# Six groups of TensorE sums in six PSUM banks instead of three groups in each of two

## The chip, the cores and the metric

The kernel runs on one core of a Trainium2 chip. The metric is the device time of one execution in microseconds (us); lower is better. Engines are called as in the profile: PE is TensorE's matmul, PEld its weight load, DVE is VectorE, ACT is ScalarE, POOL is GpSimd, SP is SyncE, which issues the stores. PSUM is the memory that matmuls write to. It has eight banks here, each with room for 512 fp32 numbers on each of 128 partitions.

## The reference, cut to what matters

Inputs are `xi` and `xj`, each 1024 x 39 x 16 (batch, field, element). For each of the 741 pairs of fields (row, column with column < row), each batch entry gets the 16 x 16 outer product of two vectors. It is normalised with a mean and a variance per pair, over the batch and both elements, and multiplied by a 16 x 16 weight:

```
cross = xj[:, rows, :, None] * xi[:, cols, None, :]
mean = jnp.mean(cross, axis=(0, 2, 3), keepdims=True)
var = jnp.mean(jnp.square(cross - mean), axis=(0, 2, 3), keepdims=True)
normed = (cross - mean) * jax.lax.rsqrt(var + BN_EPS)
normed = normed * gamma[None, :, None, None] + beta[None, :, None, None]
out = normed[:, :, None, :, :] * W[None, None, :, :, :]
```

The output is 1024 x 1 x 741 x 16 x 16 in fp32, 777 MB, so the bulk of the run is the writing of it. But nothing of the output can be finished before the mean and variance are known, and these need the whole batch.

## The kernel before, in words

The batch is laid out as 128 partitions x 8 entries; the index of the entry is called t (0 to 7). The kernel has two phases.

**Statistics.** The mean of an outer product is a product of sums: for each batch entry and field, the kernel needs only the sum over the 16 elements of `xi` and of `xj` (k = 0), and the same sum of their squares (k = 1). These sums are called moments. ACT makes the squares (`square`, L361), one field tensor and one t at a time. Then the 16 elements have to be summed, in four ways:

- `reduce` (L364): DVE sums 608 numbers per partition to 38.
- `fold` (L368) and `folded` (L371): POOL adds the upper eight elements to the lower eight, and DVE sums what is left, 304 numbers to 38.
- `matrix_sums` (L380) and `take` (L386): PE multiplies by a unit matrix and accumulates in PSUM, four of the 16 elements at a time for one t, or two at a time for two t's, so that 152 numbers per partition are left; DVE sums these to the moments. This serves k = 0 for t = 1 to 5. The groups are called `i_1`, `j_1` (t = 1), `i_23`, `j_23` (t = 2 and 3) and `i_45`, `j_45` (t = 4 and 5); `i` stands for `xi`, `j` for `xj`. For k = 0, t = 0 and 7 go by `reduce`, t = 6 by `fold` and `folded`; for k = 1 nearly all goes by `reduce`.
- `gram` (L390): PE multiplies the moments of `xj` with those of `xi` over the batch and so gets a 38 x 38 table of sums for k = 0 and one for k = 1.

All this is in a hand-written order (`tc.manual_schedule()`): each engine executes its instructions in the order in which the program lists them, and the waits between engines follow from the tiles and banks that they share. On PE the order is `i_1`, `j_1`, `i_23`, `j_23`, `i_45`, `j_45`, then the `gram` matmuls. On DVE, 28 summing instructions come one after the other: 22 reductions from SBUF with the six `take`s between them. The lines that place the groups and the first `take`s are

```
at = 2 * T * G * (n // 2)
ps = banks[5 + x][:, at : at + 2 * T * G]
...
i_1 = matrix_sums(1, 1, 2)
j_1 = matrix_sums(0, 1, 2)
i_23 = matrix_sums(3, 2, 4)
j_23 = matrix_sums(2, 2, 4)
reduce(1, 1, 1)
take(*i_1)
```

so the three `i` groups lie side by side in bank 6, the three `j` groups in bank 5, and the matmuls of `i_23` and `j_23` stand in the program ahead of `take(*i_1)`.

After the two tables, a short chain on 38 x 38 numbers gives scale and offset of each pair: ACT L461 and L462, DVE L463 to L466, ACT L468, DVE L471 to L474. `spread` (L488) copies a table row to all 128 partitions with a matmul, and `apply` (L499 to L506) multiplies with gamma and adds beta. While the statistics run, POOL and ACT also make the raw outer products of the first output tile (L150 and L148).

**Output.** The output is made in tiles: one row of the pair table and two t's each. POOL scales `xi` (L170), ACT and POOL make outer products (L148, L150), DVE adds the offset and multiplies by the weight (`finish`, L308) with a share of POOL and ACT, and SP issues the store (L231). The first tile is different: it has raw products, which get scale and offset in `affine` (ACT L245, POOL and DVE L247) and the weight in `weigh` (L254), whose first store is the kernel's first. The output lies in one large SBUF buffer (`y_sb`) used as a ring: a later tile can be written only when an earlier one's store is done.

PSUM holds the banks `ps_s` (bank 0, written by twelve warm-up matmuls at the start, L402), `ps_c` (bank 1, small tables of the chain), `ps_g` (banks 2 to 4; the first two take the tables of `gram`), banks 5 and 6, and one more bank for `w_dve`, a copy of the weight that ACT makes at L469. `spread` uses banks 5, 6 and 2 to 4 later on.

Of the kernel before, what the change touches and what calls it, by code (L numbers as in the profile page):

```python
# [14 lines left out]
T = 2  # L15
# [26 lines left out]
def tile_pair_outer_batchnorm(  # L42
# [49 lines left out]
    w_dve = psp.tile([P, 1, EE], F32, name="w_dve")  # L92
# [27 lines left out]
    G = F - 1  # L120
# [9 lines left out]
    banks = [psp.tile([P, 512], F32, name=f"ps{n}") for n in range(7)]  # L130
    ps_s, ps_c, ps_g = banks[0], banks[1], banks[2:5]
# [186 lines left out]
    with tc.manual_schedule():  # L318
# [44 lines left out]
        def reduce(x, k, t):  # L363
            nc.vector.tensor_reduce(moment(x, k, t, t + 1), field(x, k)[:, t : t + 1], AX.X, ALU.add)  # L364
# [7 lines left out]
                moment(x, k, t, t + 1), halves[k][x][:, t : t + 1], AX.X, ALU.add  # L372
            )

        def matrix_sums(n, t0, t1):
            x, q = n % 2, 2 * T // (t1 - t0)
            at = 2 * T * G * (n // 2)
            ps = banks[5 + x][:, at : at + 2 * T * G]
            for e in range(0, E, q):
                nc.tensor.matmul(  # L380
                    ps, unit, sources[x][:, t0:t1, :, e : e + q], start=e == 0, stop=e + q == E
                )
            return x, t0, t1, ps.rearrange("p (t f q) -> p t f q", t=t1 - t0, q=q)

        def take(x, t0, t1, ps):
            nc.vector.tensor_reduce(moment(x, 0, t0, t1), ps, AX.X, ALU.add)  # L386
# [23 lines left out]
        reduce(1, 1, 0)  # L410
        reduce(0, 0, 0)
        reduce(0, 1, 0)
        i_1 = matrix_sums(1, 1, 2)
        j_1 = matrix_sums(0, 1, 2)
        i_23 = matrix_sums(3, 2, 4)
        j_23 = matrix_sums(2, 2, 4)
        reduce(1, 1, 1)
        take(*i_1)
        reduce(0, 1, 1)
# [3 lines left out]
        reduce(1, 1, 3)  # L423
        reduce(0, 1, 3)
        take(*i_23)
        i_45 = matrix_sums(5, 4, 6)
        j_45 = matrix_sums(4, 4, 6)
        reduce(1, 1, 4)
        reduce(0, 1, 4)
        fold(1, 0, 6)  # L430
# [130 lines left out]
```

## Time and profile before

| | |
|---|---|
| time, median of 3 runs | 1872.28 us (1871.1 to 1872.44) |
| span of the profiled execution | 1869.4 us |
| busy: DVE, ACT, POOL | 92%, 84%, 83% of the span |
| busy: PE | 34.5 us, 2% |
| written to memory | 776.99 MB |
| moved, mean over the span | 419 GB/s |
| first store issued | 31.73 us after the start of the span |

A row of a profile's timeline gives the start in us, the duration of the row (first start to last end), engine, line, operation, output <- input with their shapes, the count, and in brackets how long the engine had been idle before it and what ended the wait. The letter q after an engine is its instruction queue. The names `ps` and `y_sb` stand for all banks, and for the ring buffer together with the small work areas laid into it.

### The profile page before, as it was taken

To read this page: it belongs to the slowest core of one execution; us is meant where nothing else is said; L and a number is where in the kernel's file an instruction comes from. 1 tells how busy PE (TensorE), PEld (TensorE's weight loads), DVE (VectorE), ACT (ScalarE), POOL (GpSimd) and SP (SyncE) were. 2 spreads that over 40 slices of the span, in tenths; PEclk is the share of its full clock that TensorE was granted. 3 is DMA by queue.
4 is the path that set the end of the run, shared out by engine and by line. 5 is a ranking of instruction groups with operands and counts; after the bars stand their busy time and mean duration, and the time that the engine had idled before them with its cause. 6 is when DMAs were issued, how large, how long until landed. Compare 5 with 4: busy or idle time off the path is not lost.

```text
span 1869.4 us, 9385 instructions
## 1 busy us (share of the span) xinstructions
PE 34.5 (2%) x212; PEld 32.9 (2%) x212; DVE 1714.5 (92%) x2638; ACT 1578.7 (84%) x3130; POOL 1546.0 (83%) x1655
## 2 busy tenths in 40 slices
PE   7000000000000000000000000000000000000000
PEld 7000000000000000000000000000000000000000
DVE  7999889899999999999999999999999999999994
ACT  7999888888888877666798989999999998989892
POOL 7999878777777788999988888888888888888882
PEclk7555555555555555555555555555555555555555
DMA  6999999999999999999999999999999999999998
GB/s 239 389 419 422 429 427 427 422 426 424 427 428 426 426 427 425 426 428 426 421 428 426 425 425 432 427 427 429 429 425 426 430 427 429 429 424 431 426 429 359
DMA packets 55286, 783.60 MB, mean 419 GB/s; under 512 B 4784, under 2 KB 6448, under 8 KB 18096
## 3 DMA queue, kind: packets, MB, share of 16 engines
q1 hardware_dynamic: 54928, 782.53, 98.8%
q14 instruction: 69, 0.57, 0.1%
q10 hardware_dynamic: 288, 0.48, 0.1%
q8 instruction: 1, 0.02, 0.0%
HBM read 6.00 MB, written 776.99 MB: 419 GB/s over the span
## 4 chain that ended last, share of the span: by engine, by line
DMA 53%; ACT 20%; DVE 16%; issue 2%; POOL 1%; SPq 0%; ACTq 0%; DVEq 0%; POOLq 0%
DMA out_dram<-y_sb 53%; ACT y_sb L148 20%; DVE y_sb L308 16%; POOL y_sb L150 0%; POOL xs L170 0%; SPq L231 0%; POOL y_sb L294 0%; DVE xs L183 0%; ACTq L148 0%; DVEq L556 0%; DVEq L308 0%; POOLq L294 0%; POOLq L150 0%
## 5 line engine op out<-in xcount | busy, mean ns | idle before, releaser
L308 DVE SCALAR_TENSOR_TENSOR y_sb<-y_sb,st_sb,w_dve 128x512 f32<-128x512 f32 (+1 forms) x2511 | 1653.1, 740 | 113.6 <-issue 96.0
L148 ACT ACTIVATE y_sb<-xs,xj_sb 128x144 f32<-128x144 f32 (+23 forms) x2930 | 1455.2, 600 | 236.2 <-DMA out_dram<-y_sb 181.4
L297 POOL TENSOR_TENSOR y_sb<-y_sb,w_sb 128x2048 f32<-128x2048 f32 (+3 forms) x155 | 517.6, 3346 | 89.0 <-ACT y_sb L292 79.4
L150 POOL TENSOR_SCALAR y_sb<-xs,xj_sb 128x320 f32<-128x320 f32 (+19 forms) x1006 | 559.6, 580 | 9.4 <-DMA out_dram<-y_sb 9.4
L170 POOL TENSOR_TENSOR xs<-xi_sb,st_sb 128x640 f32<-128x640 f32 (+33 forms) x135 | 184.1, 1364 | 176.4 <-ACT y_sb L148 172.2
L294 POOL TENSOR_SCALAR y_sb<-y_sb,st_sb 128x512 f32<-128x512 f32 x291 | 197.6, 694 | 5.1 <-ACT y_sb L148 5.1
L292 ACT ACTIVATE y_sb<-y_sb,st_sb 128x512 f32<-128x512 f32 x160 | 100.3, 710 | 3.8 <-POOL y_sb L150 2.1
L203 POOL TENSOR_TENSOR y_sb<-xs,xj_sb 128x1280 f32<-128x1280 f32 (+2 forms) x24 | 66.7, 2806 | 0.0
L193 DVE TENSOR_TENSOR y_sb<-xs,ps 128x256 f32<-128x256 f32 (+3 forms) x32 | 24.8, 817 | 0.6
L488 PE MATMUL ps<-y_sb 38*128 38x38 f32 (+37 forms) x76 | 16.4, 397 | 2.4 <-DVE y_sb L474 2.4
L488 PEld LDWEIGHTS ps<-y_sb 38*128 38x128 f32 x76 | 16.3, 329 | 2.5 <-issue 2.5
L247 POOL TENSOR_SCALAR y_sb<-y_sb,st_sb 128x512 f32<-128x512 f32 x9 | 7.0, 793 | 8.4 <-ACT y_sb L148 8.4
L150 POOL TENSOR_SCALAR y_sb<-xi_sb,xj_sb 128x304 f32<-128x304 f32 x24 | 12.0, 518 | 0.0
L254 DVE TENSOR_TENSOR y_sb<-y_sb,w_dve 128x2048 f32<-128x2048 f32 (+4 forms) x6 | 10.8, 1840 | 0.5 <-POOL y_sb L247 0.5
L364 DVE TENSOR_REDUCE y_sb<-y_sb 128x38 f32<-128x608 f32 x14 | 10.4, 779 | 0.0
L386 DVE TENSOR_REDUCE y_sb<-ps 128x76 f32<-128x152 f32 (+1 forms) x6 | 1.9, 313 | 6.5 <-PE ps L380 6.5
L461 ACT ACTIVATE y_sb<-ps 38x38 f32<-38x38 f32 x1 | 0.2, 198 | 8.0 <-PE ps L390 8.0
L361 ACT ACTIVATE y_sb<-xj_sb 128x608 f32<-128x608 f32 x8 | 5.7, 710 | 1.2 <-DMA xj_sb<-in_r_xj_dram 0.8
L245 ACT ACTIVATE y_sb<-y_sb,st_sb 128x512 f32<-128x512 f32 x9 | 6.5, 806 | 0.3 <-ACT y_sb L148 0.3
L361 ACT ACTIVATE y_sb<-xi_sb 128x608 f32<-128x608 f32 x8 | 5.7, 708 | 1.2 <-DMA xi_sb<-in_r_xi_dram 1.0
L380 PE MATMUL ps<-xi_sb,y_sb 128*128 128x152 f32 x40 | 5.9, 297 | 3.9 <-DVE y_sb L386 2.7
L380 PE MATMUL ps<-xj_sb,y_sb 128*128 128x152 f32 x40 | 5.7, 290 | 0.0
(40 smaller groups left out, 58.0 us busy)
## 6 DMA issues: line engine op xcount, KB each, us to landing
out_dram<-y_sb SPq DMA_DIRECT2D x16, 3072.0 KB, 21.9
out_dram<-y_sb SPq DMA_DIRECT2D x20, 2432.0 KB, 12.6
out_dram<-y_sb SPq DMA_DIRECT2D x10, 4608.0 KB, 15.2
out_dram<-y_sb SPq DMA_DIRECT2D x12, 3840.0 KB, 20.8
out_dram<-y_sb SPq DMA_DIRECT2D x16, 2816.0 KB, 22.0
out_dram<-y_sb SPq DMA_DIRECT2D x12, 3584.0 KB, 22.9
out_dram<-y_sb SPq DMA_DIRECT2D x12, 3328.0 KB, 24.3
out_dram<-y_sb SPq DMA_DIRECT2D x15, 2560.0 KB, 12.4
```

The lines of the kernel that those rows point to most:

```text
L148: nc.scalar.activation(y, src, AF.Copy, scale=scale)
L150: engine.tensor_scalar(y, src, scale, 1.0, ALU.mult, ALU.mult)
L170: nc.gpsimd.tensor_tensor(xs, xi_sb[:, t0 : t0 + T, 0:r, :], s_sb[:, :, n0 : n0 + r, :].to_broadcast([P, T, r, E]), ALU.mult,)
L193: nc.vector.tensor_tensor(view(n)[:, t].rearrange("p n (i j) -> p n i j", j=E), xs[:, t].unsqueeze(2).to_broadcast([P, r, E, E]), xj_short ...
L203: nc.gpsimd.tensor_tensor(view(n)[:, t].rearrange("p n (i j) -> p n i j", j=E), xs[:, t].unsqueeze(2).to_broadcast([P, r, E, E]), xj_sb[:, ...
L292: nc.scalar.activation(y[:, :, c, :], y[:, :, c, :], AF.Identity, bias=t_c)
L294: nc.gpsimd.tensor_scalar(y[:, :, c, :], y[:, :, c, :], t_c, 1.0, ALU.add, ALU.mult)
L297: nc.gpsimd.tensor_tensor(y[:, :, c0:c1, :], y[:, :, c0:c1, :], w_sb.unsqueeze(1).to_broadcast([P, T, c1 - c0, EE]), ALU.mult,)
L308: stt(y[:, t : t + size, c, :], y[:, t : t + size, c, :], t_sb[:, n0 + c : n0 + c + 1], w_dve.to_broadcast([P, size, EE]), ALU.add, ALU.mult,)
L361: nc.scalar.activation(squares[x][:, t], sources[x][:, t], AF.Square, scale=scales[x])
L380: nc.tensor.matmul(ps, unit, sources[x][:, t0:t1, :, e : e + q], start=e == 0, stop=e + q == E)
L488: nc.tensor.matmul(ps[:, :, first[r] - n0 : first[r] - n0 + r], pick[:, r - 1, :], stq[:, :, 0:r], start=True, stop=True,)
```

## The change

Each of the six groups gets a bank of its own. `matrix_sums` is told the bank, and the column offset goes away. The banks are ones that the program holds anyway, at a time when they are otherwise unused: `ps_c` before the chain, `ps_g[2]` before `spread`, `ps_s` after the warm-up, and the bank of `w_dve` before the weight is copied into it. The purpose is that a `take` should no longer share a bank with a group that PE writes around the same time. Number, shapes and order of the instructions on each engine stay as they are.

```diff
-        def matrix_sums(n, t0, t1):
-            x, q = n % 2, 2 * T // (t1 - t0)
-            at = 2 * T * G * (n // 2)
-            ps = banks[5 + x][:, at : at + 2 * T * G]
+        def matrix_sums(ps, x, t0, t1):
+            q = 2 * T // (t1 - t0)
+            ps = ps[:, 0 : 2 * T * G]
...
-        i_1 = matrix_sums(1, 1, 2)
-        j_1 = matrix_sums(0, 1, 2)
-        i_23 = matrix_sums(3, 2, 4)
-        j_23 = matrix_sums(2, 2, 4)
+        i_1 = matrix_sums(ps_c, 1, 1, 2)
+        j_1 = matrix_sums(ps_g[2], 0, 1, 2)
+        i_23 = matrix_sums(banks[5], 1, 2, 4)
+        j_23 = matrix_sums(banks[6], 0, 2, 4)
...
-        i_45 = matrix_sums(5, 4, 6)
-        j_45 = matrix_sums(4, 4, 6)
+        i_45 = matrix_sums(ps_s, 1, 4, 6)
+        j_45 = matrix_sums(w_dve[:, 0], 0, 4, 6)
```

The changed kernel is one line shorter, so its line numbers from `matrix_sums` on are lower by one: L379 is the matmul and L385 the `take`.

## Prediction

> **What bounds the kernel now.** I read the slices of the page first, to see whether one thing binds throughout.
>
> ```profile
> DVE  7999889899999999999999999999999999999994
> DMA  6999999999999999999999999999999999999998
> GB/s 239 389 419 422 429 427 427 422 426 424 427 428 426 426 427 425 426 428 426 421 428 426 425 425 432 427 427 429 429 425 426 430 427 429 429 424 431 426 429 359
> ```
>
> From the second slice on the DMA engines are busy throughout and move some 425 GB/s; the writing is the long bound. Only the first slice (47 us) stands out. So the second view is the busy time by stretch:
>
> ```profile
> 16.00:20.00 4.00, 3.99 (x30) 3.99 (x31) 2.03 (x3) 1.98 (x4) 3.73 (x7) 1.00 0.34 127
> 20.00:24.00 4.00, 1.93 (x26) 1.31 (x24) 3.52 (x8) 0.00 (x0) 2.03 (x5) 1.00 0.00 0
> 24.00:26.00 2.00, 0.74 (x8) 0.60 (x8) 2.00 (x5) 0.02 (x1) 0.00 (x0) 0.64 0.00 0
> 26.00:30.00 4.00, 1.32 (x7) 1.22 (x7) 2.05 (x11) 2.97 (x9) 0.00 (x0) 0.50 0.00 0
> ...
> 60.00:70.00 10.00, 0.00 (x0) 0.00 (x0) 9.97 (x18) 10.00 (x23) 9.65 (x13) 0.50 0.82 335
> ```
>
> (Columns: length, busy PE, PEld, DVE, ACT, POOL, PE clock, DMA share, GB/s.) Loads are over before 20 us; from 20 to 30 us nothing is moved. Ten us of the span are pure statistics, with no other work than some raw products beside them. Every us off this phase starts the store stream a us sooner.
>
> Third, the waits of the first 32 us, and fourth, the timelines of DVE and PE there:
>
> ```profile
> DVE y_sb L386 <- PE ps L380: 6.5, 3, 3.6
> PE ps L380 <- DVE y_sb L386: 2.7, 1, 2.7
> ```
>
> ```profile
> 6.15 1.47 DVE L364 TENSOR_REDUCE y_sb<-y_sb 128x38 f32<-128x608 f32 x2
> 11.26 0.32 DVE L386 TENSOR_REDUCE y_sb<-ps 128x38 f32<-128x152 f32 x1 [3.64 <-PE ps L380]
> 13.34 0.32 DVE L386 TENSOR_REDUCE y_sb<-ps 128x38 f32<-128x152 f32 x1 [0.38 <-PE ps L380]
> 15.65 0.31 DVE L386 TENSOR_REDUCE y_sb<-ps 128x76 f32<-128x152 f32 x1
> 20.48 0.32 DVE L386 TENSOR_REDUCE y_sb<-ps 128x76 f32<-128x152 f32 x1 [2.45 <-PE ps L380]
> 25.75 0.47 DVE L371 TENSOR_REDUCE y_sb<-y_sb 128x38 f32<-128x304 f32 x1
> ```
>
> ```profile
> 5.63 1.27 PE L380 MATMUL ps<-xi_sb,y_sb 128*128 128x152 f32 x8 [0.22 <-DMA xi_sb<-in_r_xi_dram]
> 6.74 1.20 PE L380 MATMUL ps<-xj_sb,y_sb 128*128 128x152 f32 x8
> 8.90 2.32 PE L380 MATMUL ps<-xi_sb,y_sb 128*128 128x152 f32 x16 [0.96 <-DMA xi_sb<-in_r_xi_dram]
> 11.06 2.24 PE L380 MATMUL ps<-xj_sb,y_sb 128*128 128x152 f32 x16
> 16.01 2.35 PE L380 MATMUL ps<-xi_sb,y_sb 128*128 128x152 f32 x16 [2.71 <-DVE y_sb L386]
> 18.20 2.24 PE L380 MATMUL ps<-xj_sb,y_sb 128*128 128x152 f32 x16
> ```
>
> The reader is to compare ends with starts. `i_1` is done at 5.63 + 1.27 = 6.90, yet its `take` starts at 11.26, just after the end of `i_23` (8.90 + 2.32 = 11.22). The `take` of `j_1` (13.34) follows the end of `j_23` (13.30), and that of `j_23` (20.48) the end of `j_45` (20.44). The other way round, `i_45` starts at 16.01, after the `take` of `i_23` ends at 15.96. So the waits are by bank, not by column: a `take` waits for the last group that stands ahead of it in the program in the same bank, though that is not its data.
>
> **What the Trainium skill says.** "PSUM — Partial Sum Buffer", section "PSUM bank collisions raise a hardware error", says that a matmul's write and another engine's access to one bank must be kept apart even at different columns, and that different banks are free. The four coincidences above agree. "Perfetto Trace Analysis", "Optimization Strategy", says to look at regimes apart and find gaps on the engine that limits a regime; here that is DVE before 26 us, not the DMA of the average. "DMA: Bandwidth & Descriptors", "Where 436 GB/s comes from", gives 435 GB/s as the ports' ceiling; the 425 to 429 here are near it, so the store stage can hardly catch up or go faster by itself. "TensorE: Matmul & The Clock Gate", "What's actually happening", says that the clock halves after an idle window of about 3.4 us; the trace has it falling between 24 and 26 us.
>
> **The change part by part.**
>
> 1. *Waits removed on DVE.* The three waits are 3.64 + 0.38 + 2.45 = 6.47 us. A wait also breaks overlap: reductions back to back start 0.70 us apart though one lasts 0.78 (two in 1.47), so each wait hides 0.08; three make 0.24. Bound: 6.7 us.
>
> 2. *Do the true inputs come in time?* I lay DVE's instructions out back to back from 6.15, where nothing changes yet, with the steps of the trace: 0.70 for a `reduce`, 0.23 for a `take`, 0.38 for a `folded`. After three reductions, the `take` of `i_1` starts at 7.54 (data 6.90); two reductions on, that of `j_1` at 9.16 (data 6.74 + 1.20 = 7.94); three on, that of `i_23` at 11.47 (data 11.22); three on, that of `j_23` at 13.77 (data 13.30). ACT's squares are single rows 0.7 to 0.8 apart, the one of `xi` for t = 6 starting at 13.51, for t = 7 at 15.13 and of `xj` at 15.94, each 0.71 long. Counting back, squares lead the DVE by 0.4 to 0.6 us at t = 3 to 5. POOL's folds for t = 6 end at 14.38, 15.18 and 15.96; DVE wants them at 14.7, 16.0 and 16.4. The fold for t = 7 ends at 17.56. All in time, the tightest by 0.2 to 0.5 us. The last reduction then starts at 19.05 in place of 25.75, and ends at 19.5: 6.7 us sooner.
>
> 3. *Wait removed on PE.* `i_45` no longer waits for a `take`. Its loads have landed: ACT squares t = 5 of `xi` at 11.99 and of `xj` at 12.74 without a DMA wait. So it follows `j_23`: groups of 16 rows start 2.16 to 2.19 apart (8.90, 11.06; 16.01, 18.20), which gives 13.22 for `i_45`, 15.4 for `j_45`, and an end at about 17.65 in place of 20.44. The `take`s of both come at 15.76 and 18.12, after these ends (15.57 and 17.65); 0.2 us is the margin for `i_45`.
>
> 4. *What stands behind the groups on PE.* The `gram` matmuls start at about 17.6. Before, 16 of their rows took 0.84 us from 20.85 on and the last eight, from the `take` of `j_45` on, 0.74 (25.20 to 25.94). Sixteen, six and eight rows, some 0.9, 0.3 and 0.74 us, end at 19.55 in place of 25.94: 6.4 us sooner. The last two follow the last reduction at 19.57 in place of 26.27: 6.7. ACT L461 starts at about 19.6, DVE L463, which needs both, at about 20.05 in place of 26.73.
>
> 5. *Waits added.* A group in `ps_s` stands behind the warm-up on the same engine, over at 5.42. The ACT write into `ps_c` (L462) comes 12 us after the `take` of `i_1`, the weight copy into `w_dve` (L469, about 21.2) after the `take` of `j_45` (18.4), and `spread` needs `ps_g[2]` later still. Nothing queues behind any of them: no cost, as the readers are long done.
>
> 6. *The rest of the first store's way.* From L463 to the first store are 31.73 - 26.73 = 5.0 us of 38 x 38 steps, ACT products and `affine`; all start from this chain. POOL's raw products end at 17.54 + 4.49 = 22.03; its `affine` would start at 30.41 - 6.7 = 23.7, so POOL isn't the new bound. Weight, gamma and beta were issued by 11.98, with landings 6.3 to 6.5 us later: 18.3. The first store goes at about 25.1.
>
> 7. *Output phase.* DVE, ACT and POOL are each 9.5 to 10 us busy in every 10 us from 40 to 160 us, the DMA at 0.98 to 1.02 from 70 us on. Nothing there depends on a clock time of its own, so it all moves. I take 6.6 us, between 6.4 and 6.7. Sum: 1872.28 - 6.6 = 1865.7 us.
>
> **The rivals.**
>
> *PE is the limit.* If only PE's own wait counts, the gain is 2.71 us: 1869.6, within 0.2%. For it: PE is busy 3.99 of 4 us from 16 to 20, and `j_45` moves only 2.8 us. Against it: after `j_45` the old DVE had 5.8 us of queued work (20.44 to 26.22), which would be done beside PE now. Squares or folds that come late would land between, at a gain of 4 to 5 us: 1867.3 to 1868.3. Chance of the two together 0.10, half of it still faster.
>
> *The lead is lost in the store stage.* The DMA queue is full for most of the run; if its pace, and not its start, fixed the end, we see 1872.3. Against it: no store is in the queue before 31.73, and the 777 MB have to pass after the first one. It could only happen where the ring's reuse falls differently against the stores. Chance 0.06.
>
> *Slower.* The earlier stream meets the compute engines at another phase, and a store is late: DMA idles 0.09 and 0.18 of the stretches at 50 and 60 us, 2.7 us in all. To end slower by 0.2% this has to grow fivefold, by 10.8 us: 1872.3 - 6.6 + 10.8 = 1876.5. One more wait as long as SP's longest for L308, 18.4 us, would give 1884. For it: all three engines are nearly full there. Against: they start together from the same trigger, and keep their order. A PE clock that halves earlier doesn't suffice: `i_45`, `j_45` and `gram` at half speed would add some 6.5 us on PE (4.4 and 2), which eats the gain but no more. Chance 0.04.
>
> **How the numbers follow.** The full gain has 0.80; run to run spread is 1.3 us, so it covers 1864 to 1867.5. Late inputs 0.10, lost lead 0.06, slower 0.04. The bound of faster by 0.2% is 1868.5. Faster: 0.80 + 0.07 = 0.87; same 0.09; slower 0.04. Range: 1863.4 (the bound of 6.7, the spread, and 0.9 for a store stage that fits better) to 1868.6 (the late inputs).
>
> **What would show it.** Right: no `take` with a PE wait over 0.3 us; the last `folded` near 19 us; ACT L460's start near 19.6 us; the first store near 25.1 us; stretches from 40 us on as before, 6.6 us earlier. Wrong: `take`s that wait for their own group, DVE idle on ACT or POOL before 19 us, POOL ending its raw products after ACT needs them, or a first store at 25 us with an end less than 4 us sooner.

## The result, and the profile after

| | before | after |
|---|---|---|
| time, median | 1872.36 us (1871.1 to 1872.75, 4 runs) | 1864.12 us (1863.88 to 1864.56, 4 runs) |
| span of the profiled execution | 1869.4 us | 1862.7 us |
| last `folded` starts | 25.75 us | 19.40 us |
| first store issued | 31.73 us | 25.32 us |

The ratio is 0.9957 (95% interval 0.994 to 0.9975). The changed kernel is 8.2 us faster by these medians, where 6.6 us was forecast. The two profiled spans differ by only 6.7 us. The gap of 1.6 us between the medians and the forecast is what the experiments had to explain, next to the mechanism itself.

First the timeline of DVE, changed kernel, cut to four `take`s, the row ahead of them and the last `folded`:

```profile
6.05 1.47 DVE L364 TENSOR_REDUCE y_sb<-y_sb 128x38 f32<-128x608 f32 x2
7.92 0.32 DVE L385 TENSOR_REDUCE y_sb<-ps 128x38 f32<-128x152 f32 x1 [0.40 <-PE ps L379]
9.54 0.31 DVE L385 TENSOR_REDUCE y_sb<-ps 128x38 f32<-128x152 f32 x1
11.84 0.31 DVE L385 TENSOR_REDUCE y_sb<-ps 128x76 f32<-128x152 f32 x1
14.14 0.31 DVE L385 TENSOR_REDUCE y_sb<-ps 128x76 f32<-128x152 f32 x1
19.40 0.47 DVE L371 TENSOR_REDUCE y_sb<-y_sb 128x38 f32<-128x304 f32 x1
```

The waits of 3.64, 0.38 and 2.45 us are gone. What is left, 0.40 us, is a wait for the `take`'s own data; it is over the 0.3 us that the prediction allowed, and the last `folded` starts 0.35 us after the forecast 19.05. The timeline of PE in the same run, cut to the warm-up, `i_1`, `i_45` and `j_45`, shows why:

```profile
1.04 5.49 PE L401 MATMUL ps<-y_sb 128*128 128x128 f32 x24 [1.04 <-POOL y_sb L319]
6.32 1.57 PE L379 MATMUL ps<-xi_sb,y_sb 128*128 128x152 f32 x8
12.92 2.25 PE L379 MATMUL ps<-xi_sb,y_sb 128*128 128x152 f32 x16
15.01 2.24 PE L379 MATMUL w_dve<-xj_sb,y_sb 128*128 128x152 f32 x16
```

The warm-up took 5.49 us here and 4.38 us in the profile before, so `i_1` came later and ended at 7.89. The clock became full later: the starts of the rows come closer together at 7.07 us here (from 0.25 to 0.13 us apart, within `i_1`), and at 4.1 us before (from 0.21 to 0.11, within the warm-up). From `i_1` on PE runs without a gap into the `gram` matmuls: `i_45` starts at 12.92, no longer after a `take`. Its clock fell earlier than before, which the stretches show (columns: length, busy PE, PEld, DVE, ACT, POOL, PE clock, DMA share, GB/s; the clock column says 1.00 for the slow rows of the first few us too, so there only the rows themselves tell):

```profile
16.00:20.00 4.00, 2.74 (x42) 2.35 (x40) 3.87 (x9) 2.40 (x7) 3.78 (x8) 1.00 0.34 122
20.00:24.00 4.00, 1.58 (x9) 1.50 (x9) 2.11 (x11) 2.49 (x8) 1.81 (x5) 0.59 0.00 0
24.00:26.00 2.00, 2.00 (x11) 2.00 (x11) 1.97 (x3) 2.00 (x3) 2.00 (x3) 0.50 0.03 8
26.00:30.00 4.00, 4.00 (x21) 4.00 (x21) 3.76 (x3) 4.00 (x7) 4.00 (x6) 0.50 0.75 278
...
53.60:63.60 10.00, 0.00 (x0) 0.00 (x0) 9.97 (x19) 10.00 (x23) 9.58 (x13) 0.50 0.82 335
```

From 16 to 20 us DVE is now busy 3.87 us, where it was 2.03. The last line, 6.4 us earlier than the stretch from 60 to 70 before, has the same DMA share and bandwidth: the output phase is the old one, moved.

### The profile page after: what moved, and what is told of

It is laid out like the page before. It is cut to its first block, busy times and chain, and to the rows that moved or that the text cites. A ratio compares the mean times of both kernels' runs of the same rounds, so it can differ in the third digit from the quotient of the medians.

```text
span 1862.7 us, 9385 instructions
## 1 busy us (share of the span) xinstructions
PE 34.3 (2%) x212; PEld 33.7 (2%) x212; DVE 1714.3 (92%) x2638; ACT 1576.3 (85%) x3130; POOL 1542.9 (83%) x1655
## 4 chain that ended last, share of the span: by engine, by line
DMA 53%; ACT 22%; DVE 18%; issue 3%; POOL 1%; PE 0%; SPq 0%; ACTq 0%; DVEq 0%; POOLq 0%
DMA out_dram<-y_sb 53%; ACT y_sb L148 22%; DVE y_sb L308 17%; POOL y_sb L150 1%; DVE y_sb L364 0%; POOL xs L170 0%; POOL y_sb L247 0%; PE ps L401 0%; SPq L231 0%; DVE y_sb L254 0%; ACTq L148 0%; PE ps L379 0%; DVE y_sb L385 0%; DVE y_sb L371 0%; DVE xs L183 0%
## 5 line engine op out<-in xcount | busy, mean ns | idle before, releaser
L379 PE MATMUL ps<-xi_sb,y_sb 128*128 128x152 f32 x40 | 6.1, 302 | 0.0
L379 PEld LDWEIGHTS ps<-xi_sb,y_sb 128*128 128x128 f32 x40 | 5.8, 202 | 0.0
L401 PE MATMUL ps<-y_sb 128*128 128x128 f32 x24 | 5.5, 428 | 1.0 <-POOL y_sb L319 1.0
L401 PEld LDWEIGHTS ps<-y_sb 128*128 128x128 f32 x24 | 5.2, 331 | 1.0 <-POOL y_sb L319 1.0
```

Source lines behind the costliest of these rows:

```text
L379: nc.tensor.matmul(ps, unit, sources[x][:, t0:t1, :, e : e + q], start=e == 0, stop=e + q == E)
```

## The experiments

The theory on trial: the end moves one for one with the first store; the first store moves with DVE's summing queue; that queue lost time to waits that the sharing of banks made, not the data. The rivals: PE is the limit; the store stage swallows or adds time; sharing a bank costs in itself.

### Only the first two groups apart

`i_1` and `j_1` keep banks of their own; the later pairs share banks 5 and 6, in different columns. (Here and in the next experiment `matrix_sums` takes a column offset again, which the cut doesn't show.)

```diff
-        i_45 = matrix_sums(ps_s, 1, 4, 6)
-        j_45 = matrix_sums(w_dve[:, 0], 0, 4, 6)
+        i_45 = matrix_sums(banks[5], 1, 4, 6, 2 * T * G)
+        j_45 = matrix_sums(banks[6], 0, 4, 6, 2 * T * G)
```

> Only the two groups for t = 1 have banks of their own; the pairs for t = 2, 3 and t = 4, 5 share banks 5 and 6 again. Theory (DVE waits by bank, and its queue is the path): the first two takes need not wait, but the take of j_23 waits for the end of j_45 (17.3 us in the changed kernel), about 3.1 us; PE itself does not wait, as the take of i_23 is over before PE is free. Last folded starts near 22.5 us, first store near 28.4 us, time some 3.1 us over the changed kernel: 1867.2 us. Rival (PE is the limit, only the end of j_45 counts): as the changed kernel, 1864.1 us.

Measured: 1867.88 us (1867.61 to 1868.28, 12 runs), ratio to the kernel before 0.9979 (0.9971 to 0.9987). First the `take` of `j_23` on DVE's timeline, then the last `folded`, then `i_45` and `j_45` on PE's:

```profile
17.24 0.32 DVE L385 TENSOR_REDUCE y_sb<-ps 128x76 f32<-128x152 f32 x1 [3.48 <-PE ps L379]
...
22.52 0.46 DVE L371 TENSOR_REDUCE y_sb<-y_sb 128x38 f32<-128x304 f32 x1
```

```profile
12.88 2.25 PE L379 MATMUL ps<-xi_sb,y_sb 128*128 128x152 f32 x16
14.96 2.24 PE L379 MATMUL ps<-xj_sb,y_sb 128*128 128x152 f32 x16
```

PE runs its groups at the same moments as in the changed kernel, with no wait, and `j_45` ends at 17.20. Still the kernel is 3.8 us slower, with DVE waiting 3.48 us for the end of a group it doesn't read there. The first store is at 28.42, as the theory had it; the time is 0.7 us over the expectation, in part because the wait is 3.48 us and not 3.1. That PE's end alone counts is ruled out.

### Only the last two groups apart

```diff
-        i_1 = matrix_sums(ps_c, 1, 1, 2)
-        j_1 = matrix_sums(ps_g[2], 0, 1, 2)
+        i_1 = matrix_sums(banks[5], 1, 1, 2, 2 * T * G)
+        j_1 = matrix_sums(banks[6], 0, 1, 2, 2 * T * G)
```

> Only the two groups for t = 4, 5 have banks of their own; t = 1 shares with t = 2, 3. Theory: the takes of i_1 and j_1 wait for the ends of i_23 and j_23 as before (about 3.3 and 0.4 us), the wait of 2.45 us before the take of j_23 is gone. Last folded starts near 23.2 us in place of 19.40 and 25.75, first store near 29.1 us, time some 3.8 us over the changed kernel: 1867.9 us. Rival (PE is the limit): PE has no wait here, so as the changed kernel, 1864.1 us.

Measured: 1868.22 us (1868.03 to 1869.13, 16 runs), ratio 0.9982 (0.9975 to 0.999). The first two waits are back (DVE timeline):

```profile
11.22 0.32 DVE L385 TENSOR_REDUCE y_sb<-ps 128x38 f32<-128x152 f32 x1 [3.77 <-PE ps L379]
...
13.30 0.32 DVE L385 TENSOR_REDUCE y_sb<-ps 128x38 f32<-128x152 f32 x1 [0.38 <-PE ps L379]
...
23.17 0.46 DVE L371 TENSOR_REDUCE y_sb<-y_sb 128x38 f32<-128x304 f32 x1
```

The first store comes at 29.16, the last `folded` at 23.17: within 0.1 us of the expectation (the time is 0.3 us over it). The losses against the changed kernel, 3.8 us in the first experiment and 4.2 here, add to more than the 6.7 us between the first two spans: with the early waits gone, DVE comes to the `take` of `j_23` sooner and waits 3.48 us there, where it waited 2.45.

### Two banks, another order

The banks and columns of before, but each `take` stands in the program ahead of the next group in its bank.

```diff
-        i_23 = matrix_sums(3, 2, 4)
-        j_23 = matrix_sums(2, 2, 4)
         reduce(1, 1, 1)
         take(*i_1)
+        i_23 = matrix_sums(3, 2, 4)
...
         take(*j_1)
+        j_23 = matrix_sums(2, 2, 4)
...
-        j_45 = matrix_sums(4, 4, 6)
...
         take(*j_23)
+        j_45 = matrix_sums(4, 4, 6)
```

> Two banks as before, at the columns of before, but each take stands in the program ahead of the next group in its bank. Theory (what costs is which instructions stand between a group and its take, not the number of banks): each take then waits for its own group alone, and the next group waits for the take; by the times of the changed kernel each take ends 0.5 to 1 us before PE comes to that group, so nothing waits. Last folded near 19.4 us, first store near 25.3 us, 1864.1 us within 0.5. Rival (sharing a bank costs in itself, whatever the order): takes or groups wait again, 2 us or more, up to 1872.3 us.

Measured: 1864.24 us (1864.09 to 1864.52, 5 runs), ratio 0.996 (0.9947 to 0.9972); first store at 25.23. The changed kernel gave 1864.03 on the same chip. The first four `take`s on DVE's timeline, then the groups after `j_1` on PE's:

```profile
7.85 0.32 DVE L386 TENSOR_REDUCE y_sb<-ps 128x38 f32<-128x152 f32 x1 [0.45 <-PE ps L380]
9.47 0.31 DVE L386 TENSOR_REDUCE y_sb<-ps 128x38 f32<-128x152 f32 x1
11.77 0.31 DVE L386 TENSOR_REDUCE y_sb<-ps 128x76 f32<-128x152 f32 x1
14.07 0.31 DVE L386 TENSOR_REDUCE y_sb<-ps 128x76 f32<-128x152 f32 x1
```

```profile
8.69 2.24 PE L380 MATMUL ps<-xi_sb,y_sb 128*128 128x152 f32 x16
10.77 2.24 PE L380 MATMUL ps<-xj_sb,y_sb 128*128 128x152 f32 x16
12.85 2.25 PE L380 MATMUL ps<-xi_sb,y_sb 128*128 128x152 f32 x16
14.94 2.24 PE L380 MATMUL ps<-xj_sb,y_sb 128*128 128x152 f32 x16
```

The 0.45 us is again a wait for `i_1` itself, in a run whose clock became full late (6.92 us). So more banks are one way to the gain and no condition of it, and that sharing a bank costs in itself is ruled out. Each engine's order is unchanged here too; what differs is which accesses come ahead of which in the program, and so who waits for whom. Each group has a `take` of its bank ahead of it now, but that `take` ends 0.5 to 1.0 us before the group starts (8.17 and 8.69 for the first pair).

One thing these runs don't tell: every bank is one tile of the program here, so a wait that goes by the bank and one that goes by the tile look alike. In SBUF the work areas share one tile, `y_sb`, and there columns are told apart: in the changed kernel DVE reads squares back to back from 9.76 to 11.92 us while ACT writes other squares into `y_sb` beside it.

### The changed kernel again

> The changed kernel as it is, as the measure for the others on the same chip. Theory (the lead at the first store is all there is, 6.4 to 6.7 us): 6.2 to 7.0 us under the kernel before. Rival (the store stage adds a gain of its own of about 1.6 us, as the first medians suggest): 7.8 to 8.6 us under it.

Measured: 1864.03 us (1863.84 to 1864.2, 5 runs) against 1871.81 (27 runs), ratio 0.9958 (0.9945 to 0.9972): 7.8 us, at the edge of the rival's expectation. But its own trace doesn't support a gain in the store stage: the first store at 24.86 and the span of 1862.1 leave 1837.2 us from first store to end, against 1837.7 in the first profile of the kernel before (1869.4 - 31.73) and 1837.4 to 1837.5 in three further ones.

The two sets of times themselves gave the clue. The changed kernel spreads over 0.4 us; the kernel before falls into two groups. Over the 69 runs of it beside these experiments, 27 lie at 1870.5 to 1871.4 us, median 1870.86, and 42 at 1871.8 to 1874.3, median 1872.57. The first have a mean granted clock of 0.507 in 24 of 27; the second 0.506 in all 42. PE's clock is full only in the statistics phase, so a lower mean says that it was full for a shorter time there (0.001 of the mean is 0.001 x 1870 / 0.5 = 3.7 us of it). All four profiles of the kernel before are of the lower group, for which the shares give a chance of only 0.02 (0.39 to the fourth power); whether profiled executions differ from the others was not tested.

### PE kept busy in the kernel before

Eight matmuls that nobody reads stand in PE's gap of 2.7 us ahead of `i_45`. All waits of DVE stay.

```diff
         take(*i_23)
+        for _ in range(8):
+            nc.tensor.matmul(ps_s[:, 0:P], ones, ones, start=True, stop=True)
         i_45 = matrix_sums(5, 4, 6)
```

> The kernel before, with eight more unit matmuls (128x128, into ps_s, read by nobody) on PE between j_23 and i_45, where PE idles 2.7 us. All waits of DVE stay. Theory (the kernel before has two groups of times, about 1870.8 us at a mean clock of 0.507 and 1872.4 at 0.506, since the idle PE lets the clock halve earlier, and i_45 and j_45 then run slower): with the gap filled only the lower group is left, median 1870.7 us, all runs within 0.6, clock 0.507. Rival (the two groups come from the store stage or the loads): both groups stay, 1870.5 to 1872.8.

Measured: 1870.99 us, and all 13 runs within 1870.73 to 1871.19. The upper group is gone, by useless work alone. PE's timeline shows the filling and `i_45`, which still waits for its `take`:

```profile
12.97 1.94 PE L427 MATMUL ps<-y_sb 128*128 128x128 f32 x16
15.84 2.35 PE L380 MATMUL ps<-xi_sb,y_sb 128*128 128x152 f32 x16 [0.93 <-DVE y_sb L386]
```

The first store is at 31.56 us, as in profiles of the lower group (31.52 to 31.73).

### The kernel before, profiled again

> The kernel before once more, for a profile of the other group of its times. Theory: if this run takes over 1871.8 us, the full clock ends before 20.4 us and the matmuls of j_45 (or i_45 too) take over 2.5 us for 16 rows in place of 2.24, so that j_45 ends 1 to 1.7 us later than at 20.44; if it takes under 1871.3, PE's rows are as in the first profile. Rival: PE's rows are the same in both.

> As the look before it: over 1871.8 us goes with a full clock that ends early and slower rows of j_45, under 1871.3 with rows as in the first profile.

> A third look at the kernel before. Theory: over 1871.8 us goes with a full clock that ends before 20.4 us and with rows of i_45 or j_45 that are slower than 2.3 us for 16; under 1871.3 with rows as in the first profile.

Measured: 1870.78, 1870.8 and 1870.88 us, all of the lower group, PE's rows as in the first profile, the clock full until after 24 us. None showed the upper group, so its matmuls were not seen directly in this kernel. These profiles do show how the gap lies when the clock stays full; the last section uses that.

### The kernel before with a cold PE

One warm-up matmul instead of twelve.

```diff
-        for _ in range(12):
+        for _ in range(1):
             nc.tensor.matmul(ps_s[:, 0:P], ones, ones, start=True, stop=True)
```

> The kernel before with one warm-up matmul in place of twelve, so that PE is idle until 5.6 us. Theory (in the kernel before, PE rows at half clock lie on the path, which makes the upper group of its times): the clock rises later, or falls over the idle gap, and rows of i_45 and j_45 run at some 0.21 us (the pace of the first 14 warm-up rows in the first profile, 2.96 us) in place of 0.14; j_45 ends 1 to 2.5 us later, time 1872.0 to 1875 us, above the lower group of 1870.8. Rival (PE's clock has no part in the upper group): 1870.8 and 1872.4 as before.

Measured: 1873.71 us (1871.24 to 1874.49, 12 runs; two of them, 1871.24 and 1871.40, lie near the lower group). This profile has what those of the kernel before lack. PE's timeline and the stretches around the gap:

```profile
11.57 2.24 PE L380 MATMUL ps<-xj_sb,y_sb 128*128 128x152 f32 x16
16.52 3.76 PE L380 MATMUL ps<-xi_sb,y_sb 128*128 128x152 f32 x16 [2.71 <-DVE y_sb L386]
20.12 2.24 PE L380 MATMUL ps<-xj_sb,y_sb 128*128 128x152 f32 x16
```

```profile
13.00:16.00 3.00, 0.82 (x7) 0.58 (x5) 2.62 (x5) 2.64 (x5) 2.61 (x4) 1.00 1.04 401
16.00:20.00 4.00, 3.48 (x16) 3.48 (x17) 2.55 (x5) 1.80 (x4) 3.72 (x8) 0.57 0.33 123
20.00:24.00 4.00, 3.59 (x39) 3.09 (x37) 1.60 (x4) 0.00 (x0) 1.84 (x4) 1.00 0.02 4
```

PE was at full clock up to the gap, idled 2.71 us, and the clock was down to 0.57 in the mean of the next 4 us: `i_45` took 3.76 us where it takes 2.35. That puts `j_45`, and with it the `take` of `j_23`, 1.4 us later. The first store is at 33.65, 1.9 us after 31.73; the other 0.5 us were lost ahead of the gap, as `i_45` starts at 16.52 and not at 16.01.

### The changed kernel with a cold PE

The same edit in the changed kernel.

> The changed kernel with one warm-up matmul in place of twelve. Theory (no idle gap on PE, and only 0.2 to 0.9 us between its groups and their takes): rows before the clock rises are slower, i_1 and j_1 still fit before the loads of i_23 at 8.8 us, later groups come up to 1.5 us late: 1864.1 to 1865.6 us, with less spread than the cold kernel before. Rival (PE became the limit): 1866 us or more.

Measured: 1864.66 us (1864.61 to 1865.01, 4 runs), first store at 25.41. Against the 1864.03 of the changed kernel, from another chip, a late clock costs 0.6 us where there is no gap, and these four runs lie within 0.4 us.

### A plain delay

```diff
-        reduce(1, 1, 7)
+        for _ in range(16):
+            reduce(1, 1, 7)
```

> The changed kernel with the reduction of the squares of xi for t = 7 made sixteen times instead of once: 15 more on DVE, 0.70 us each, 10.5 us, after all takes and with no bank shared. Theory (the end moves with the first store, one for one, whatever delays it): last folded near 29.7 us, first store near 35.6 us, 1864.1 + 10.5 = 1874.6 us. Rival (the store stage takes up a part of a lead or a delay): 1870 us or less.

Measured: 1876.29 us (1876.13 to 1876.41, 12 runs). The size was missed: each repeat took 0.82 us, not 0.70, as the one row shows (it reads and writes the same places as the one ahead; which of the two counts was not tested):

```profile
18.13 13.09 DVE L364 TENSOR_REDUCE y_sb<-y_sb 128x38 f32<-128x608 f32 x16
...
31.14 0.46 DVE L371 TENSOR_REDUCE y_sb<-y_sb 128x38 f32<-128x304 f32 x1
```

But the relation holds: the first store is at 37.11, 12.25 us after that of the changed kernel in its second profile (24.86), and the time rose by 1876.29 - 1864.03 = 12.26 us. The store stage neither swallows nor adds.

### Two more folds

Two DVE reductions of 0.70 us become a POOL fold and a DVE reduction of 0.38 us each; one raw product of POOL is put off for it.

```diff
         reduce(0, 1, 4)
+        fold(1, 1, 5)
         fold(1, 0, 6)
...
-        emit(raw0_pool, 1)
+        fold(1, 1, 7)
         fold(0, 1, 7)
-        reduce(1, 1, 5)
         take(*j_23)
+        folded(1, 1, 5)
...
-        reduce(1, 1, 7)
+        folded(1, 1, 7)
```

> The changed kernel with two reductions of 608 numbers (squares of xi, t = 5 and t = 7) cut into a fold on POOL and a reduction of 304 on DVE. Theory (DVE's queue is the path of the statistics now): 2 x (0.70 - 0.38) = 0.64 us less on DVE, POOL has 2.2 us to spare before its affine and idles 0.6 us before the folds; last folded 0.6 us sooner, time 1863.5 us. Rival (PE or the loads have become the limit with the change): no change, 1864.1 us, or later where a fold comes late.

Measured: 1863.98 us (1863.83 to 1864.05, 5 runs) against 1864.03, from another chip: no difference that can be told. From DVE's timeline, then ACT's and POOL's:

```profile
11.75 1.47 DVE L364 TENSOR_REDUCE y_sb<-y_sb 128x38 f32<-128x608 f32 x2
13.34 0.32 DVE L385 TENSOR_REDUCE y_sb<-ps 128x76 f32<-128x152 f32 x1
13.68 0.47 DVE L371 TENSOR_REDUCE y_sb<-y_sb 128x38 f32<-128x304 f32 x1
...
23.09 0.55 DVE L247 TENSOR_SCALAR y_sb<-y_sb,st_sb 128x512 f32<-128x512 f32 x1 [0.21 <-ACT y_sb L148]
```

```profile
21.13 1.86 ACT L148 ACTIVATE y_sb<-xi_sb,xj_sb 128x304 f32<-128x304 f32 x4
```

```profile
12.81 0.83 POOL L368 TENSOR_TENSOR y_sb<-y_sb 128x304 f32<-128x304 f32 x1
```

The `take` of `j_23` could start at 13.1 by DVE's queue and starts at 13.34, as its group ends at 13.29; `folded` at 13.68 starts as POOL's fold ends (13.64); further on DVE waits for ACT's raw products. The first store came at 24.51, only 0.35 us sooner, and even that isn't found at the end. In this trace PE, POOL and ACT all stand within a few tenths of a us of DVE; the 0.64 us taken off DVE's queue brought nothing.

## Why the prediction was right, and where it fell short

- *Step 1, DVE's waits.* Right. Undoing either half brings the named waits back (3.77 and 0.38 us; 3.48 us), with the time that belongs to them.
- *Step 2, inputs in time.* Right but for `i_1`. The second profile of the changed kernel had its `take`s at 7.49, 9.10, 11.40, 13.70, 15.69 and 18.04 us, all within 0.1 us of the forecast from the back-to-back steps. (From 6.15 on these steps start with two reductions, not three; the sum is right.) Where the clock became full late, `i_1` came late and its `take` waited 0.40 or 0.45 us for its own group, a sign that the prediction had put down as one of being wrong. It had read the pace of the warm-up from one profile.
- *Steps 3 and 4, PE and `gram`.* Right at the ends: `i_45` at 12.92 for 13.22, ACT L460 at 19.38 for 19.6. Between them two sizes were off. The 0.84 us for 16 `gram` rows is the row of the weight loads; the matmuls of the profile before took 0.96. And the last eight rows came after a wait of 0.68 us and took 0.48 us, where 0.74 without a wait was forecast. That L460 is off by only 0.2 us is in part luck.
- *Step 5, no new waits.* Right: none of them shows in the trace.
- *Step 6, the first store.* Forecast 25.1; 25.32 and 24.86 in two profiles.
- *Step 7, the output phase moves whole.* Right. Over fourteen profiles, with first stores from 24.51 to 37.11 us, the rest of the span was 1837.2 to 1837.7 us.
- *The sum* was 1.6 us short. The term that failed is the 1872.28 us from which the 6.6 us were taken. That is a median, while the 6.6 us were read from a profile of a run of 1871.38 us, in which PE's clock stayed full over the gap. What the gap does to the clock in the other runs stood in the sum at nothing; "A PE clock that halves earlier" was weighed for the changed kernel alone. The three times before, 1871.1, 1872.28 and 1872.44, which the prediction took for a spread of 1.3 us, already hold the two groups. In 42 of 69 runs of the kernel before the time was 1.7 us higher, at a lower mean clock. Against the lower group the change brings 1870.86 - 1864.03 = 6.8 us, close to the sum; against the upper 1872.57 - 1864.03 = 8.5. That a clock which halves over the gap slows `i_45` is shown by the cold kernel, and that the gap makes the upper group by the filled one. That it is `i_45` in the upper group itself was not profiled; an estimate in the last section gives the same size.
- *The rivals.* PE as the limit fell with the first two experiments, the lost lead with the delay, and slower with the result. The two-bank order adds what the prediction hadn't seen: the same gain needs no further bank.

## What to carry to other kernels

When a reader starts just as a matmul group ends that isn't its own, look for a shared bank and for what stands ahead of the reader in the program: moving the reader up can serve as well as another bank. In a phase that holds back everything after it, each us counts whole, however small its share; but after the largest wait is gone, look at all engines of the phase before trimming one. A gap on PE costs more than its length if the clock falls in it, and one profile need not show that: compare the spread and the granted clocks of several runs, and take a saving that was read from a profile off the time of that same run.

## What was not expected of the hardware

- The clock changes on a grid of 3.41 us. In the cold kernel before it rises at 9.21 us, falls at 16.04, rises at 19.45 and falls at 26.28; in all fourteen traces a stretch of full clock lasts a multiple of 3.41 us (6.83, 13.65, 17.07 or 20.48). The grid lies differently in each run: with twelve warm-up matmuls the clock becomes full at 3.91 to 7.07 us. "TensorE: Matmul & The Clock Gate", "What's actually happening", names windows of about 3.4 us that are free-running, and these traces agree.
- The same section lets the clock halve after an idle window; here the window need not be wholly idle, and the gap of 2.71 us is shorter than one. First the three windows around the gap in the cold kernel before, then the two that share the gap in the third further profile of the kernel before:

```profile
12.62:16.04 3.42, 1.20 (x10) 0.96 (x8) 3.04 (x6) 3.06 (x5) 2.77 (x5) 1.00 1.04 402
16.04:19.45 3.41, 2.93 (x11) 2.93 (x12) 2.51 (x5) 1.76 (x4) 3.13 (x7) 0.50 0.37 140
19.45:22.86 3.41, 3.27 (x28) 3.00 (x28) 0.46 (x2) 0.00 (x0) 2.39 (x5) 1.00 0.02 5
```

```profile
11.62:15.03 3.41, 1.54 (x12) 1.31 (x11) 3.03 (x6) 3.06 (x6) 2.69 (x5) 1.00 1.05 409
15.03:18.44 3.41, 2.57 (x19) 2.57 (x20) 2.86 (x5) 2.72 (x5) 3.17 (x7) 1.00 0.68 253
```

After a window with 1.20 us of matmuls the clock was half for the next one; after one with 1.54 us it stayed full. (This holds for the wide rows here. With rows of 38 columns it fell after 1.62 us of them, from 17.31 to 20.72 us in the changed kernel.) An estimate from these figures: for the clock to stay full, neither part of the gap may be longer than a limit between 3.41 - 1.54 = 1.87 and 3.41 - 1.20 = 2.21 us. If the grid lies at random, that is so in (2 x 1.87 - 2.71) / 3.41 = 0.30 to (2 x 2.21 - 2.71) / 3.41 = 0.50 of the runs; 27 of 69, 0.39, were in the lower group. And one window of half clock takes at most 3.41 / 2 = 1.7 us of work from PE; the groups are 1.71 us apart. So where the grid falls against the gap would account for the share and the size of the upper group. No run sets the grid, and five of the 42 times, 1873.18 to 1874.27, lie higher than one such window explains.
- Sixteen reductions that read and write the same places again and again start 0.82 us apart; those of the summing queue, each with places of its own, 0.70.
